# Order of work in an attention loop: the probabilities' transposes a unit later, behind the maxima; the masks' sums behind the normalisation two units back

## The chip, the cores and the metric

The kernel runs on one core of one Trainium2 chip. The metric is the device time of one execution in microseconds (us). A core has four compute engines that work from queues of their own: TensorE (PE in the profile, its weight loads PEld), VectorE (DVE), ScalarE (ACT) and GpSimd (POOL). SyncE (SP) issues all of this kernel's transfers.

## What is computed

Two layers of a gated cross-attention block, on x of shape 8 x 128 x 512 and a context of the same shape. The change lies in the attention of the first layer: 32 heads of width 128, with a position bias per head and a mask per batch.

```
h_q = (rmsnorm(hidden) @ w_q.T).reshape(b, lq, H, DH)      # H = 32, DH = 128
h_k = (context @ w_k.T).reshape(b, lk, H, DH)
h_v = (context @ w_v.T).reshape(b, lk, H, DH)
score = einsum('bqhd,bkhd->bhqk', h_q, h_k) + position_bias[None]
score = where(m, score, -inf)
score = where(m, softmax(score), 0)
attn = einsum('bhqk,bkhd->bqhd', score, h_v).reshape(b, lq, H * DH)
x = x + tanh(g) * (hidden + attn @ w_out.T)
```

After it come a 4-bit quantised dense layer, a second attention of one head and a dense layer with eight low-rank experts.

## The kernel before

The program is unrolled in full. It has three stages. First all keys and queries are projected, pair of heads by pair of heads, and stored in DRAM (to about 350 us). Then comes a loop over 64 units, in which values are projected, attention is done and the output projection is added to x (about 350 to 835 us). Last come the remaining layers, as a pipeline over the eight batches.

A unit is one head and one half of the batch, that is 4 batches: `where(u)` gives head and half. Values (`make_values`, matmuls named c_v at L172 to L174) and output projections (`project_out`, matmuls named pso at the same lines, added into x at L702) are spread over the units as they are needed. For one unit u the attention itself goes like this:

- `fetch(u + 2)` loads the stored queries and keys two units ahead (L552).
- `add_masks(u)`, L615, on GpSimd: the mask (0 or a huge negative number) plus the head's bias into a tile of tag s. There are 3 buffers of s.
- `attend(u - 3)`, L683 on TensorE: probabilities times values for the unit three back; its result is split into two parts on ScalarE (L684) and VectorE (L685).
- `scores(u, s)`: four products of queries and keys (L627, TensorE), their sum with the masks (L628, VectorE), the negated maxima of the rows (L632, VectorE), four exponentials with row sums (L639, ScalarE), the reciprocal and its product with a 0/1 factor, named rs (L644 and L645, VectorE), and the normalisation of the whole tile by rs (L646, GpSimd).
- `move_probs(u)`: the tile goes out to DRAM as through (L657) and comes back in four pieces as moved (L660), with blocks exchanged between partitions. There are 2 buffers of moved.
- `transpose_probs(u - 1)`, L668, on VectorE: each 32 x 32 block of the moved tile is transposed into pT, of which there are 2 buffers. Together with the move this is the transpose of the probabilities.

The engines' queues do not simply follow the program's text. When the program is built, a scheduler with a timeline of its own lays out each engine's queue: among what it holds ready at a moment it takes what stands first in the text. Two tools bend this order. `mark(name, inst)` notes an instruction, and `with behind(name):` makes every instruction in the block queue behind the noted one on the same engine. It adds an order within that queue, no wait for anything else. `in_order` keeps one engine's queue as the text has it; it is used on TensorE around the first and the last stage, not around the units. So the place of `transpose_probs(u - 1)` is: on VectorE, somewhere behind rs of unit u. The mask sums have no such order: a mask sum may be queued as soon as the scheduler sees a buffer of s come free, that is when through of the unit three back has left.

The last attends (units 61 to 63) and the last transpose (unit 63) are in `ending()`, the first of the last stage's steps.

Of the kernel before, what the change touches and what calls it, by code (L numbers as in the profile page):

```python
# [13 lines left out]
ALU = mybir.AluOpType  # L14
AX = mybir.AxisListType

P = 128
# [5 lines left out]
NU = 2 * H  # L23
HALF = NB // 2
BY_PAIR = [b for j in range(HALF) for b in (j, j + HALF)]
NR = 15
Q32 = 32
NQ = P // Q32
# [32 lines left out]
def kernel(  # L61
# [37 lines left out]
    nc = tc.nc  # L99
# [6 lines left out]
    def keep(shape, name, dtype=F32):  # L106
        return sb.tile(shape, dtype, tag=name, name=name)

    def slot(shape, tag, name, dtype=F32):
        return sb.tile(shape, dtype, tag=tag, name=name, bufs=TAGS[tag])  # L110
# [9 lines left out]
    def ptile(shape, tag, name):  # L120
        return psum.tile(shape, F32, tag=tag, name=name, bufs=BANKS[tag])
# [8 lines left out]
    def mark(name, inst):  # L130
        marks[name] = inst.ins

    @contextmanager
    def behind(*names):
        with ExitStack() as stack:
            for name in names:
                stack.enter_context(tc.issue_after(marks[name]))
            yield
# [206 lines left out]
    def load_wo(h):  # L345
        if h < H:
            load(f"wo_{h}", wo[:, h])

    def split_wo(h):
        t = raws.pop(f"wo_{h}")  # L350
        high, low = (wide_row("wo", f"wo_{n}{h}", F32R) for n in "hl")
        split(high, low, t, nc.gpsimd)
        wos[h] = high, low
# [3 lines left out]
    def load_bias(g):  # L357
        if g < NP:
            t = slot([P, 2, P], "bias", f"bias_{g}")
            nc.sync.dma_start(out=t, in_=pbias[:, g * 2 : (g + 1) * 2])  # L360
            biases[g] = t
# [184 lines left out]
    def fetch(u):  # L546
        if u < NU:
            p, r = divmod(u, 4)
            half, i = divmod(r, 2)
            for kind in ("queries", "keys"):  # L550
                t = slot([P, HALF * P], "kq", f"{kind[0]}_{u}")
                nc.sync.dma_start(out=t, in_=stored[kind, p][:, 2 * i + half])  # L552
                fetched[kind, u] = t
# [16 lines left out]
    def by_block(t):  # L570

        return t.rearrange("p b (n k) -> p n b k", k=Q32)
# [3 lines left out]
    mneg = keep([P, 2, NQ, HALF, Q32], "mneg")  # L576
# [27 lines left out]
    def where(u):  # L604

        p, r = divmod(u, 4)
        half, i = divmod(r, 2)
        return 2 * p + i, half

    def add_masks(u):  # L610

        h, half = where(u)
        s = slot([P, NQ, HALF, Q32], "s", f"s_{u}")
        bias = biases[h // 2][:, h % 2, :].rearrange("p (n k) -> p n k", k=Q32)
        nc.gpsimd.tensor_tensor(  # L615
            s, mneg[:, half], bias.unsqueeze(2).to_broadcast([P, NQ, HALF, Q32]), ALU.add
        )
        return s

    def scores(u, s):  # L620
        _, half = where(u)
        q, k = fetched.pop(("queries", u)), fetched.pop(("keys", u))
        bs = slice(half * HALF, (half + 1) * HALF)
        ps = ptile([P, HALF, P], "sc", f"sc_{u}")
        for j in range(HALF):
            cols = bass.ts(j, P)
            nc.tensor.matmul(ps[:, j, :], lhsT=q[:, cols], rhs=k[:, cols], start=True, stop=True)  # L627
        nc.vector.tensor_tensor(s, by_block(ps), s, ALU.add)  # L628
        nm = small.tile([P, HALF], F32, tag="nm", name=f"nm_{u}")
        mark(  # L630
            "max",
            nc.vector.tensor_reduce(  # L632
                nm, s.rearrange("p n b k -> p b n k"), AX.XY, ALU.max, negate=True
            ),
        )
        sm = small.tile([P, HALF], F32, tag="sm", name=f"sm_{u}")
        for j in range(HALF):
            one = s[:, :, j, :]
            e = nc.scalar.activation(  # L639
                one, one, AF.Exp, bias=nm[:, j : j + 1], accum_out=sm[:, j : j + 1]  # L640
            )
        mark("exp", e)
        rs = small.tile([P, HALF], F32, tag="rs", name=f"rs_{u}")
        nc.vector.reciprocal(rs, sm)  # L644
        mark("rs", nc.vector.tensor_tensor(rs, rs, anykey[:, bs], ALU.mult))  # L645
        nc.gpsimd.tensor_tensor(  # L646
            s, s, rs.unsqueeze(1).unsqueeze(3).to_broadcast([P, NQ, HALF, Q32]), ALU.mult
        )
        probs[u] = s

    def move_probs(u):


        s = probs.pop(u)
        moved = slot([P, NQ, HALF, Q32], "moved", f"moved_{u}")
        through = dram.tile([P, NQ, HALF * Q32], F32, tag="through", name=f"through_{u}")
        nc.sync.dma_start(out=through, in_=s.rearrange("p n b k -> p n (b k)"))  # L657
        blocks = through.rearrange("(i q) n f -> n q i f", q=Q32)
        for j in range(NQ):
            nc.sync.dma_start(  # L660
                out=moved[bass.ts(j, Q32)].rearrange("p i b k -> p i (b k)"), in_=blocks[j]
            )
        probs[u] = moved

    def transpose_probs(u):

        t = slot([P, HALF, P], "pT", f"pT_{u}")
        nc.vector.transpose(by_block(t), probs[u])  # L668
        probs[u] = t

    def attend(u):
        h, half = where(u)
        p, i = divmod(h, 2)
        pT = probs.pop(u)
        if i == 0:
            attns[p, half] = page([P, 2, 2, HALF, P], f"a_{p}_{half}")
        a = attns[p, half][:, i]
        ah, al = a[:, 0], a[:, 1]
        cols = bass.ts(i, P)
        av = ptile([P, HALF, P], "av", f"av_{u}")  # L680
        for b in range(HALF):
            v = values_of[p, half, b // 2][:, b % 2, :]
            nc.tensor.matmul(av[:, b, :], lhsT=v[:, cols], rhs=pT[:, b, :], start=True, stop=True)  # L683
        mark("a", nc.scalar.copy(ah, av))  # L684
        nc.vector.tensor_tensor(al, av, wide(ah), ALU.subtract)  # L685
# [19 lines left out]
    def project_out(p, b):  # L705
        half, j = divmod(b, HALF)
        ps = ptile([P, D], "mm", f"pso_{p}_{b}")
        product(
            ps,
            [  # L710
                (tuple(attns[p, half][:, i, part, j, :] for part in range(2)), wos[2 * p + i])
                for i in range(2)
            ],
        )
        add_to_x(b, ps, tgx0, "h1" if p == NP - 1 else None)
# [218 lines left out]
    def make_values(n):  # L934
        nonlocal made
        while made < n:
            next(value_work, None)
            made += 1

    def unit(u):  # L940
        p, r = divmod(u, 4)
        fetch(u + 2)
        if r == 3:
            load_bias(p + 1)
        if r in (0, 1):
            load_wo(2 * p + r)

        n = 2 * (u - OUT_LAG)

        goal = 14 + int(1.74 * (u - 2)) if u > 2 else 0  # L950
        if n >= 0:
            project_out(*divmod(n, NB))
        make_values((made + goal + 1) // 2)
        if n >= 0:
            project_out(*divmod(n + 1, NB))
        make_values(goal)
        s = add_masks(u)
        if u >= LAG:
            attend(u - LAG)
        scores(u, s)  # L960
        move_probs(u)
        if u > 0:
            with behind("rs"):
                transpose_probs(u - 1)
        if r in (2, 3):
            with behind("exp"):
                split_wo(2 * p + r - 2)

    make_values(7)
    unit(0)  # L970
    make_values(11)
    unit(1)
    make_values(14)
    for u in range(2, NU):
        unit(u)
# [299 lines left out]
    def ending():  # L1275

        outs = iter(range(2 * (NU - OUT_LAG), NP * NB))

        def project(n):
            for _ in range(n):  # L1280
                project_out(*divmod(next(outs), NB))

        project(4)
        attend(NU - 3)
        project(1)
        yield
        project(3)
        make_values(14 * (H // 4 + 1) - 3)
        attend(NU - 2)
        yield  # L1290
        make_values(14 * (H // 4 + 1))
        transpose_probs(NU - 1)
        yield
        attend(NU - 1)
        project(4)
        yield

    key, ffn, att, last = ([s(b) for b in range(NB)] for s in (keys, ffn0, xattn1, ffn1))

    starts = [[ending()], ffn[:1], ffn[1:2], ffn[2:3], [ffn[3], key[0]]]  # L1300
    starts += [[ffn[b], key[b - 3]] for b in range(4, NB)]
    starts += [[att[0], key[5]], [att[1], key[6]], [att[2], key[7]]] + [[c] for c in att[3:] + last]
# [76 lines left out]
```

## Time and profile before

| what | value |
|---|---|
| time, median of 3 runs | 973.51 us (970.68 to 974.13) |
| the profiled execution | 976.74 us, of which the span from first to last instruction is 974.9 us |
| matmul clock granted | 0.991 on average |
| DMA, mean over the span | 180 GB/s |
| first and last scores of the loop (L627) | from 350.4 us, unit 63's at 814.2 us |
| transposes (L668) | 64, 0.71 us each, 372.9 to 828.0 us |
| mask sums (L615) | 64, 1.29 us each, 292.5 to 803.6 us |
| normalisations (L646) | 64, 1.04 us each, 360.5 to 820.2 us |
| through<-s, moved<-through | 2.7 and 2.5 us from issue to landing (median) |

The profile is of one execution. A line of it names an engine, a line of the kernel, an operation, and the tiles as out<-in. Behind the bar stand the busy time, the mean length of one instruction in ns, and the idle time of the engine ahead of these instructions with what ended it. In a timeline, the idle time ahead of an instruction and its releaser stand in square brackets.

### The profile page before, as it was taken

What the parts mean: (1) busy time and instruction counts of PE and PEld (TensorE: products, weight loads), DVE (VectorE), ACT (ScalarE), POOL (GpSimd) and SP (SyncE); (2) the same over time, 40 slices, a digit from 0 to 9 for tenths busy, and PEclk for the clock granted to TensorE, in tenths of its full rate; (3) what the DMA queues carried; (4) which work ended last, traced back from release to release, by engine and by line L of the source; (5) the groups of instructions that cost most, each with busy time, mean ns of one, the idle gap of its engine ahead of it and who ended that gap; (6) DMA issues with size and microseconds to landing.
All of it is one profiled execution on the core that took longest, in us unless ns stands there. A gap on an engine that the chain in (4) does not pass through costs nothing. (4 is left out here: it accounts for less than half of the span.)

```text
span 974.9 us, 16587 instructions
## 1 busy us (share of the span) xinstructions
PE 926.1 (95%) x5444; PEld 807.9 (83%) x5444; DVE 651.5 (67%) x1341; ACT 500.0 (51%) x1435; POOL 482.4 (49%) x524
## 2 busy tenths in 40 slices
PE   6989999998999988899999999999999999989998
PEld 4877788887888878799889989898898998878987
DVE  7777766675778944665667576575676577645686
ACT  5565545655564544443434445353552535666761
POOL 4844322112231584763847649376495852553431
PEclk9999999999999999999999999999999999999999
DMA  8544465788886687566665856656575656513001
GB/s 282 176 143 131 141 204 180 229 262 279 275 273 202 200 255 221 156 192 166 178 179 174 222 166 181 195 166 193 160 205 171 174 160 205 216 45 131 1 23 66
DMA packets 125269, 175.00 MB, mean 180 GB/s; under 512 B 17406, under 2 KB 55294, under 8 KB 124030
## 3 DMA queue, kind: packets, MB, share of 16 engines
q1 hardware_dynamic: 125182, 173.94, 58.4%
q8 instruction: 43, 0.70, 0.3%
q14 instruction: 44, 0.36, 0.1%
HBM read 109.85 MB, written 64.03 MB: 178 GB/s over the span
## 5 line engine op out<-in xcount | busy, mean ns | idle before, releaser
L639 ACT ACTIVATE s<-s,nm 128x128 f32<-128x128 f32 x256 | 99.7, 391 | 188.0 <-issue 76.0
L615 POOL TENSOR_TENSOR s<-mneg,bias 128x512 f32<-128x512 f32 x64 | 82.5, 1291 | 87.1 <-DMA through<-s 78.3
L172 PE MATMUL pso<-wo_h,a 128*128 128x512 f32 x256 | 107.2, 419 | 6.1 <-DVE x L702 6.1
L668 DVE STREAM_TRANSPOSE pT<-moved 128x512 f32<-128x512 f32 x64 | 45.4, 710 | 97.7 <-DMA moved<-through 97.4
L174 PE MATMUL pso<-wo_h,a 128*128 128x512 f32 x256 | 101.2, 396 | 1.1 <-DVE a L685 1.1
L173 PE MATMUL pso<-wo_l,a 128*128 128x512 f32 x256 | 101.1, 395 | 0.0
L646 POOL TENSOR_TENSOR s<-s,rs 128x512 f32<-128x512 f32 x64 | 66.6, 1041 | 64.6 <-ACT wo_h L163 18.7
L702 DVE SCALAR_TENSOR_TENSOR x<-pso,tg,x 128x512 f32<-128x512 f32 x128 | 93.4, 738 | 5.7 <-PE pso L174 5.7
L172 PE MATMUL c_v<-wvP,cxT 128*128 128x256 f32 x288 | 82.6, 287 | 0.8 <-ACT v L253 0.7
L173 PE MATMUL c_v<-wvP,cxT 128*128 128x256 f32 x288 | 81.5, 283 | 0.0
L174 PE MATMUL c_v<-wvP,cxT 128*128 128x256 f32 x288 | 81.4, 283 | 0.0
L683 PE MATMUL av<-pT,v 128*128 128x128 f32 x512 | 69.1, 276 | 8.0 <-DVE pT L668 6.0
L683 PEld LDWEIGHTS av<-pT,v 128*128 128x128 f32 x512 | 64.5, 191 | 13.2 <-issue 5.3
L627 PE MATMUL sc<-k,q 128*128 128x128 f32 x512 | 69.9, 279 | 4.2 <-issue 1.6
L627 PEld LDWEIGHTS sc<-k,q 128*128 128x128 f32 x512 | 64.2, 194 | 6.1 <-DVE nm L632 2.9
L172 PE MATMUL c_v<-wvP,cxB 128*128 128x256 f32 x216 | 61.8, 286 | 3.4 <-DVE v L254 2.6
L172 PEld LDWEIGHTS pso<-wo_h,a 128*128 128x128 f32 x256 | 48.5, 189 | 15.2 <-DVE x L702 6.6
L173 PE MATMUL c_v<-wvP,cxB 128*128 128x256 f32 x216 | 61.0, 283 | 0.0
L174 PE MATMUL c_v<-wvP,cxB 128*128 128x256 f32 x216 | 61.0, 282 | 0.0
L164 POOL TENSOR_TENSOR wvP<-raw_wv,wvP 128x512 fp32r<-128x512 f32 x43 | 56.3, 1318 | 7.1 <-ACT wvP L163 7.1
L174 PEld LDWEIGHTS pso<-wo_h,a 128*128 128x128 f32 x256 | 48.0, 188 | 13.0 <-DVE a L685 2.0
L172 PEld LDWEIGHTS c_v<-wvP,cxT 128*128 128x128 f32 x288 | 55.0, 191 | 4.0 <-ACT v L253 1.3
(276 smaller groups left out, 2779.9 us busy)
## 6 DMA issues: line engine op xcount, KB each, us to landing
keys<-keys SPq DMA_DIRECT2D x64, 256.0 KB, 3.4
queries<-queries SPq DMA_DIRECT2D x64, 256.0 KB, 3.9
q<-queries SPq DMA_DIRECT2D x64, 256.0 KB, 4.0
k<-keys SPq DMA_DIRECT2D x64, 256.0 KB, 4.5
through<-s SPq DMA_DIRECT2D x64, 256.0 KB, 2.7
moved<-through SPq DMA_DIRECT2D x256, 64.0 KB, 2.5
raw_wk<-in_wk_dram SPq DMA_DIRECT2D x32, 256.0 KB, 3.9
raw_wq<-in_wq_dram SPq DMA_DIRECT2D x32, 256.0 KB, 4.1
```

The costliest lines, as they stand in the source:

```text
L164: mark("low", (low_engine or nc.vector).tensor_tensor(low, src, wide(high), ALU.subtract))
L172: nc.tensor.matmul(out, lhsT=lh, rhs=rh, start=first, stop=False, **more)
L173: nc.tensor.matmul(out, lhsT=lh, rhs=rl, start=False, stop=False, **more)
L174: nc.tensor.matmul(out, lhsT=ll, rhs=rh, start=False, stop=last, **more)
L615: nc.gpsimd.tensor_tensor(s, mneg[:, half], bias.unsqueeze(2).to_broadcast([P, NQ, HALF, Q32]), ALU.add)
L627: nc.tensor.matmul(ps[:, j, :], lhsT=q[:, cols], rhs=k[:, cols], start=True, stop=True)
L639: e = nc.scalar.activation(one, one, AF.Exp, bias=nm[:, j : j + 1], accum_out=sm[:, j : j + 1])
L646: nc.gpsimd.tensor_tensor(s, s, rs.unsqueeze(1).unsqueeze(3).to_broadcast([P, NQ, HALF, Q32]), ALU.mult)
L668: nc.vector.transpose(by_block(t), probs[u])
L683: nc.tensor.matmul(av[:, b, :], lhsT=v[:, cols], rhs=pT[:, b, :], start=True, stop=True)
L702: "x", nc.vector.scalar_tensor_tensor(xs[b], ps, factor, xs[b], ALU.mult, ALU.add, **out)
```

## The change

The transposes are called a unit later and from inside `scores`: unit u's call follows the maxima of unit u + 2, and has to queue behind them on VectorE. What was called for unit 62 in unit 63 is now called in the ending. The mask sum of unit u has to queue behind the normalisation of unit u - 2 on GpSimd. Nothing is computed otherwise.

```
     def add_masks(u):
...
-        nc.gpsimd.tensor_tensor(
-            s, mneg[:, half], bias.unsqueeze(2).to_broadcast([P, NQ, HALF, Q32]), ALU.add
-        )
+        with behind(*(f"norm{u - 2}",) * (u > 1)):
+            nc.gpsimd.tensor_tensor(
+                s, mneg[:, half], bias.unsqueeze(2).to_broadcast([P, NQ, HALF, Q32]), ALU.add
+            )
         return s
...
     def scores(u, s):
...
         mark("max", nc.vector.tensor_reduce(nm, ..., AX.XY, ALU.max, negate=True))
+        if u > 1:
+            with behind("max"):
+                transpose_probs(u - 2)
         sm = small.tile([P, HALF], F32, tag="sm", name=f"sm_{u}")
...
-        nc.gpsimd.tensor_tensor(
-            s, s, rs.unsqueeze(1).unsqueeze(3).to_broadcast([P, NQ, HALF, Q32]), ALU.mult
-        )
+        factors = rs.unsqueeze(1).unsqueeze(3).to_broadcast([P, NQ, HALF, Q32])
+        mark(f"norm{u}", nc.gpsimd.tensor_tensor(s, s, factors, ALU.mult))
         probs[u] = s
...
         scores(u, s)
         move_probs(u)
-        if u > 0:
-            with behind("rs"):
-                transpose_probs(u - 1)
...
     def ending():
...
         project(3)
+        transpose_probs(NU - 2)
         make_values(14 * (H // 4 + 1) - 3)
         attend(NU - 2)
```

## The prediction

> **What bounds the kernel now.** I read the page's busy table first, then the busy times by stage, then TensorE's waits in the stage that the change touches, and last the timeline of VectorE and GpSimd inside it.
>
> ```profile
> PE 926.1 (95%) x5444; PEld 807.9 (83%) x5444; DVE 651.5 (67%) x1341; ACT 500.0 (51%) x1435; POOL 482.4 (49%) x524
> ...
> L615 POOL TENSOR_TENSOR s<-mneg,bias 128x512 f32<-128x512 f32 x64 | 82.5, 1291 | 87.1 <-DMA through<-s 78.3
> ...
> L668 DVE STREAM_TRANSPOSE pT<-moved 128x512 f32<-128x512 f32 x64 | 45.4, 710 | 97.7 <-DMA moved<-through 97.4
> ```
>
> TensorE is busy nearly all the time and VectorE two thirds of it. The two groups that the change moves are the two that hold their engines longest for a DMA: the mask sums on GpSimd (78.3 us) and the transposes on VectorE (97.4 us). Idle time of an engine that is not the bound is worth nothing by itself; the question is what it does to TensorE. By stage (columns: length, then PE, PEld, DVE, ACT, POOL busy, clock, DMA share, GB/s):
>
> ```profile
> 350.00:400.00 50.00, 41.81 (x306) 38.95 (x304) 23.68 (x48) 25.07 (x88) 30.08 (x26) 0.97 0.78 231
> 400.00:835.00 435.00, 421.54 (x2852) 382.93 (x2853) 287.61 (x516) 197.28 (x655) 269.68 (x235) 1.00 0.62 179
> ```
>
> The units run from about 350 us (scores of unit 0) to 835 us. From 400 to 835 us TensorE is idle 435.00 - 421.54 = 13.5 us. Its waits there add up to exactly that, and all end on VectorE:
>
> ```profile
> PE av L683 <- DVE pT L668: 5.6, 5, 1.3
> PE pso L172 <- DVE x L702: 5.3, 8, 2.7
> PE c_v L172 <- DVE v L254: 2.6, 3, 1.4
> ```
>
> So 13.5 us, 1.4% of the run, is all that a better order of VectorE can win in this stage. One of these waits, read in the timeline of VectorE (columns: start, length, engine, line, operation, count, idle before and who ended it):
>
> ```profile
> 569.37 0.74 DVE L702 SCALAR_TENSOR_TENSOR x<-pso,tg,x 128x512 f32<-128x512 f32 x1
> 572.15 0.71 DVE L668 STREAM_TRANSPOSE pT<-moved 128x512 f32<-128x512 f32 x1 [2.03 <-DMA moved<-through]
> 572.78 0.65 DVE L254 TENSOR_TENSOR v<-c_v,v 128x512 f32<-128x512 f32 x1
> 573.36 0.68 DVE L685 TENSOR_TENSOR a<-av,a 128x512 fp32r<-128x512 f32 x1
> 573.96 0.68 DVE L628 TENSOR_TENSOR s<-sc,s 128x512 f32<-128x512 f32 x1
> ```
>
> and the matmul that paid for it, in TensorE's:
>
> ```profile
> 573.49 0.39 PE L172 MATMUL c_v<-wvP,cxB 128*128 128x256 f32 x1 [1.44 <-DVE v L254]
> ```
>
> The transpose of unit 28 waits 2.03 us for its DMA. The value sum at L254 and unit 30's score sum at L628 stand behind it, although unit 30's scores had been multiplied from 567.5 us on. TensorE waits 1.44 us for the value sum. GpSimd shows the same shape:
>
> ```profile
> 563.75 1.04 POOL L646 TENSOR_TENSOR s<-s,rs 128x512 f32<-128x512 f32 x1 [1.33 <-ACT a L684]
> 566.97 1.27 POOL L615 TENSOR_TENSOR s<-mneg,bias 128x512 f32<-128x512 f32 x1 [2.18 <-DMA through<-s]
> 569.60 1.04 POOL L646 TENSOR_TENSOR s<-s,rs 128x512 f32<-128x512 f32 x1 [1.35 <-ACT v L253]
> ```
>
> The sum at 566.97 is unit 31's mask, three units ahead of the normalisation at 563.75 (unit 28), because the three buffers of tag s make it wait until unit 28's probabilities have left.
>
> **What the Trainium skill says.** "TensorE: Matmul & The Clock Gate", section "Architectural detail: the array is 16× 32×32, not 1× 128×128": VectorE and GpSimd take their instructions strictly in order. The trace agrees: the 2.03 us above. "Perfetto Trace Analysis", section "Identifying the Most-Contended Engine": TensorE's headroom is judged by the weight loads' busy share, not the matmuls'. Here that is 382.93 of 435.00, 88%, so I do not take TensorE's 97% as a wall, only as saying that its queue seldom runs dry. "DMA: Bandwidth & Descriptors", section "Two DMAs through the same engine are not ordered": a DMA that reads what another wrote has to be issued after the first one's semaphore. The trace shows the issuing queue doing so: SyncE's queue waits 84.1 us, 55 times, at L660 for the DMA through<-s between 400 and 835 us. This makes the round trip that a transpose waits for two DMAs long.
>
> **The change, part by part.**
>
> (1) The transposes. The number stays 64, each 0.71 us, all on VectorE. Unit u's moves from behind rs(u+1) to behind the maxima of unit u+2. In the timeline, over units 9 to 61 (the steady ones), the maxima come every 7.4 us. The moved block of unit u has landed on average 11.9 us after the end of u's maxima (0.3 until the exponentials, 1.6 for four of them, 1.0 to rs, 0.7 to the normalisation of 1.04, 0.2 to the issue of through, 3.0 to that of moved, 4.1 to the landing). The old slot, behind rs(u+1), is at 7.4 + 2.9 = 10.3 us, so the transpose is early by 1.6 us on average and VectorE waits. The new slot is at 14.4 us, 2.5 us after the mean landing. Most of the 97 us should go; by the same readings 15 to 30 us stay where landings are late (one in ten lands 15.3 us or more after the maxima).
>
> What that wins on TensorE: the three value waits, 2.6 us, each directly behind a waiting transpose. Of the eight x waits, 5.3 us, one of 2.7 us at 402 us belongs to the start, where DMA landings set the order, and one of 0.6 us at 818 us to the end; 2.0 us are left to win. The five pT waits, 5.6 us, are no matter of slot: the DMA itself was late. Two of them (units 16 and 17, 2.2 us) should shrink as the whole softmax chain moves up when VectorE no longer holds it: I take 1.5. Three (units 34, 42, 50, 3.4 us) follow a pair of scores only 2.3 us apart. There a mask sum (1.3 us each) stands ahead of the late normalisation on GpSimd, as at 604.7 us before the normalisation of unit 34 at 608.7, and the change puts it behind: I take 2.2. Sum won: 2.6 + 2.0 + 1.5 + 2.2 = 8.3 us.
>
> What it costs: the result is needed by attend(u), which TensorE runs just ahead of the scores of unit u+3. Now 2.6 us lie on average between the transpose's end and it; with the new slot less. From the end of the scores of u+2 to attend(u) there are on average 5.8 us. The new path in them is the score sum 0.68, the maxima 0.69 and the transpose 0.71, with 0.1 to 0.15 at each step about 2.4 us, plus whatever else VectorE has in its queue ahead of them. So some 3.4 us of other work fit. I bounded the shortfall from both sides over the 53 units. If the score sum starts within 1.4 us of its matmuls' end (two other operations ahead), 0.2 us of waits in three units. If it starts when it did, less only the idle time of the transpose directly ahead of it, 9.7 us in 11 units (unit 27: transposed by 567.7 us, wanted at 566.6). The second forgets that earlier waits pushed it too: the score sum now comes 4.2 us after the first score matmul, of which 1.1 are the matmuls. I take 3 us, near the lower end, as the waits were what pushed it. Behind the moved transpose stand one x or value sum and rs; rs has 1.6 us of exponentials as cover for its 0.71.
>
> (2) The mask sums. 64 stay, 1.29 us each. Unit u's is put behind the normalisation of u-2, whose unit's maxima come before; the buffer it waits for (unit u-3's) has then been free for some 4 us, so 66 us of GpSimd's waits between 400 and 835 us go. It is wanted by the score sum of u. From the end of normalisation u-2 to that sum there are now 8.6 us on average and 4.1 at the least (unit 34), against 1.3 for the mask: covered, unless splits of weights (1.3 us each) line up three deep. At the start mask 2 moves from 347.8 to behind normalisation 0 (361.5 us) and comes out 0.5 us late for its sum at 362.3; mask 5 likewise 0.8 us. Both sums stand in the stretch up to 400 us whose order the DMAs' landings set, so I take 0, and keep 1.4 as the other end. No queue of SyncE waits for a mask.
>
> (3) The buffers. Block u+2 is moved into the buffer that transpose u frees; its DMA is issued some 7 us after the maxima of u+2, the transpose comes 0.7 us after them: no wait. pT: transpose u needs attend(u-2), a unit earlier. The last two transposes come in the ending; unit 62's now in program order behind three output projections, with its DMA landed at 823.9 us and attend(62) at 832.9: nothing.
>
> Sum: -8.3 + 3 + 0 = -5.3 us. The profiled execution took 976.7 (span 974.9), which would become 971.4; it lay 3.2 above the median of the runs shown, 973.5, for which the same sum gives 968.
>
> **The rivals.** A wash (B): the order edges bind little, or the time won comes back as waits at attend. For it: at units 33, 41, 49 and 57 the transpose already comes after the maxima of u+2 (602 to 611 us: no change there), as in most of the first six units; and the upper bound of the cost, 9.7, against 8.3 won. Against: in the other 49 of 53 units the transpose stands ahead of those maxima. Time 971 to 977, say 974.
>
> Slower (C): TensorE closes a loop. Scores of u+2, their sum, maxima, transpose of u, attend(u), scores of u+3 are one chain now, of 4.3 us without queueing in a period of 7.4. If one VectorE operation more (0.7 us) stands ahead of the sum than in my upper bound, the same reading gives 19.4 us of waits in 17 units, less the 4.6 us of x and value waits won: +15, 988 us; with half of one (0.35 us), 13.8 - 4.6 = +9, 983 us. It decides where the score sum starts on average some 2.2 us or more after its matmuls' end (my upper bound has 1.9; traced are 3.1). For it: VectorE has 3.5 us of other work per unit, and the scheduler that lays out the queues rearranges everything with the edges. Against: this queueing is now made by the very waits that go.
>
> **How the numbers follow.** The forecast (A) 0.60, its own range 963 (10.7 of the 13.5 us won) to 972 (4.6 won, 3 lost). B 0.14. C 0.26, 979 to 990. A measurement tells about 0.5%, 4.9 us, from no change: under 968.6 lie 0.43 of A and 0.01 of B; within 968.6 to 978.4 0.17 of A, 0.11 of B, 0.01 of C; above, 0.25 of C and 0.02 of B. Low end 961, below A's own by what the start might give; high end 985, inside C.
>
> **What would show it.** Right: the wait of the transposes falls from 97 to under 35 us, that of the mask sums to under 15; the score sum starts within 3 us of its first matmul; TensorE's waits for L254 and x after 410 us are gone; waits at attend total 5 us or less. Wrong: attend waits for the transposes in 15 or more units (C), or the transposes keep over 60 us of waits (B). A changed order on TensorE itself, attends behind the next scores, would make the sum above unsafe in both directions.

## The result and the profile after

The changed kernel takes 960.33 us, median of 4 runs (955.06 to 962.43), against 972.18 us (970.68 to 974.13) for the kernel before, measured beside it: 11.9 us less, a ratio of 0.987 with a 95% interval of 0.982 to 0.992. The forecast was 968 from a median of 973.5 then, a gain of 5.3, so the gain has the right sign and is about twice as large as forecast. The profiled execution of the changed kernel took 959.39 us (span 957.6). The pair of profiled executions differs by 17.3 us, 5.5 more than the medians do: the one before lay 4.6 above its median, this one 0.9 below. Differences between the two traces are therefore not a measure of the gain to the microsecond.

The page of the changed kernel, its busy table and the two groups that moved:

```profile
PE 919.2 (96%) x5444; PEld 807.4 (84%) x5444; DVE 650.3 (68%) x1341; ACT 505.9 (53%) x1435; POOL 482.4 (50%) x524
...
L616 POOL TENSOR_TENSOR s<-mneg,bias 128x512 f32<-128x512 f32 x64 | 82.5, 1289 | 26.4 <-DMA through<-s 26.4
...
L671 DVE STREAM_TRANSPOSE pT<-moved 128x512 f32<-128x512 f32 x64 | 45.2, 706 | 46.3 <-DMA moved<-through 46.3
```

Counts and lengths of the instructions are the same as before. The mask sums' wait for a DMA falls from 78.3 to 26.4 us, the transposes' from 97.4 to 46.3. The same stretch of the units as in the prediction, now 13 us shorter (columns as there):

```profile
350.00:400.00 50.00, 43.41 (x304) 41.03 (x303) 29.25 (x55) 25.69 (x89) 27.40 (x24) 0.93 0.74 222
400.00:822.00 422.00, 414.75 (x2848) 381.47 (x2847) 284.13 (x513) 203.33 (x655) 270.20 (x234) 1.00 0.63 188
```

From 400 to 822 us TensorE shows 422.00 - 414.75 = 7.3 us of idle time, where it showed 13.5 before. Again its waits add up to that (columns: engine, line and what it is waiting for; us in total, times, longest):

```profile
PE av L686 <- DVE pT L671: 4.6, 4, 2.1
PE pso L172 <- DVE x L705: 2.0, 1, 2.0
PE c_v L172 <- ACT v L253: 0.7, 1, 0.7
```

The value waits are gone, one x wait near the end of the loop is left, and attends wait 4.6 us instead of 5.6. So the named waits fell by 6.2 us, close to the 5.3 of the forecast, and yet the kernel won about twice that. The timeline of VectorE in the changed kernel, at the place that the prediction showed (L629 is the score sum, L633 the maxima, L671 the transpose):

```profile
573.34 0.69 DVE L688 TENSOR_TENSOR a<-av,a 128x512 fp32r<-128x512 f32 x1 [2.42 <-ACT a L687]
573.95 0.68 DVE L629 TENSOR_TENSOR s<-sc,s 128x512 f32<-128x512 f32 x1
574.80 0.75 DVE L705 SCALAR_TENSOR_TENSOR x<-pso,tg,x 128x512 f32<-128x512 f32 x1 [0.17 <-PE pso L174]
575.47 0.67 DVE L633 TENSOR_REDUCE nm<-s 128x4 f32<-128x512 f32 x1
576.06 0.70 DVE L671 STREAM_TRANSPOSE pT<-moved 128x512 f32<-128x512 f32 x1
```

The transpose of unit 30 follows the maxima of unit 32 without a wait: its block has been there for a while. What VectorE waits for here is an attend's result, which comes when TensorE gets to it and holds nobody up.

GpSimd's timeline in the changed kernel (L651 a normalisation, L616 a mask sum):

```profile
579.70 1.04 POOL L651 TENSOR_TENSOR s<-s,rs 128x512 f32<-128x512 f32 x1 [0.33 <-DVE rs L649]
...
581.95 1.30 POOL L616 TENSOR_TENSOR s<-mneg,bias 128x512 f32<-128x512 f32 x1
...
584.45 1.03 POOL L651 TENSOR_TENSOR s<-s,rs 128x512 f32<-128x512 f32 x1
585.45 1.29 POOL L616 TENSOR_TENSOR s<-mneg,bias 128x512 f32<-128x512 f32 x1
```

Normalisations 32 and 33 are each followed by the mask sum of two units on, 34 and 35, and these find their buffer free.

**Where the rest of the gain was.** The prediction read TensorE's lost time from its idle column. Two matmuls of the kernel before, and the next one, in TensorE's timeline:

```profile
571.42 0.39 PE L173 MATMUL pso<-wo_l,a 128*128 128x512 f32 x1
571.65 0.40 PE L174 MATMUL pso<-wo_h,a 128*128 128x512 f32 x1
573.49 0.39 PE L172 MATMUL c_v<-wvP,cxB 128*128 128x256 f32 x1 [1.44 <-DVE v L254]
```

The first two start 0.23 us apart, although each is shown with 0.39 to 0.40 us: matmuls are pipelined, and 0.23 us is what one of 512 columns costs. The third starts 1.84 us after the second, so 1.61 us are lost, and the idle column says 1.44. Each gap is understated by some 0.17 us (the shown length less the distance), and a gap shorter than that isn't shown at all. I therefore took the usual (median) distance from one start to the next for each kind of matmul (227 ns for 512 columns, 120 for 256, 111 for 128, 122 for 264), which makes about 895 us of issued work in every kernel of this study, and called loss what a stretch of issued work takes beyond that. From 400 to 835 us the kernel before issued 411.1 us of work: its loss is 23.9 us, not 13.5. Of that, 9.6 us lie in 97 gaps of more than 0.05 us that are too short for the idle column. The changed kernel issues the same matmuls with a loss of 12.0. By stretches of issued work, in us (these count work and not time: 400 is reached at 443 us before and 436 after, 750 at 812 and 795):

| stretch of issued work | before | changed |
|---|---|---|
| 0 to 325 (first stage) | 27.6 | 24.6 |
| 325 to 400 (start of the unit loop) | 14.9 | 11.3 |
| 400 to 750 (steady units) | 19.2 | 9.1 |
| 750 to 835 (end of the loop) | 10.2 | 10.0 |
| 835 to the end | 7.5 | 7.2 |

The steady units give 10.1 us and the start of the loop 3.6. The 3.0 us of the first stage aren't the change's: no matmul of it moved, and the other kernels of the study lie between 23.2 and 27.7 there. The granted clock differs there as well, 0.99 before and 1.00 after; at the start of the loop it is 0.98 before and 0.96 after, so it doesn't explain the gain there. In the steady units it is 1.00 in both (columns as above):

```profile
443.00:812.00 369.00, 358.64 (x2443) 326.46 (x2441) 245.09 (x436) 164.61 (x558) 230.52 (x193) 1.00 0.63 180
436.00:795.00 359.00, 354.39 (x2446) 326.66 (x2445) 243.03 (x441) 171.88 (x568) 232.29 (x194) 1.00 0.62 186
```

The first line is before, the second after. Over these same matmuls the idle time falls from 10.4 to 4.6 us, the loss by distances from 19.2 to 9.1.

### The profile page after: what moved, and what is told of

Its sections match the earlier page's. It is cut to its first block, busy times and chain, and to the rows that moved or that the text cites. A ratio compares the mean times of both kernels' runs of the same rounds, so it can differ in the third digit from the quotient of the medians.

```text
span 957.6 us, 16579 instructions
## 1 busy us (share of the span) xinstructions
PE 919.2 (96%) x5444; PEld 807.4 (84%) x5444; DVE 650.3 (68%) x1341; ACT 505.9 (53%) x1435; POOL 482.4 (50%) x524
## 4 chain that ended last, share of the span: by engine, by line
PE 63%; DMA 14%; DVE 11%; issue 4%; POOL 3%; ACT 2%; SPq 2%; DVEq 0%; POOLq 0%; ACTq 0%
PE sc L628 5%; PE pso L174 5%; PE pso L172 5%; PE av L686 5%; PE pso L173 5%; PE c_v L172 4%; PE c_v L173 4%; PE c_v L174 4%; DMA raw_wk<-in_wk_dram 4%; DMA through<-s 4%; PE c_q L172 3%; PE c_q L174 3%; PE c_q L173 3%; DMA moved<-through 2%; PE c_k L172 2%
## 5 line engine op out<-in xcount | busy, mean ns | idle before, releaser
L651 POOL TENSOR_TENSOR s<-s,rs 128x512 f32<-128x512 f32 x64 | 66.7, 1043 | 100.0 <-DVE rs L649 64.5
L616 POOL TENSOR_TENSOR s<-mneg,bias 128x512 f32<-128x512 f32 x64 | 82.5, 1289 | 26.4 <-DMA through<-s 26.4
L628 PE MATMUL sc<-k,q 128*128 128x128 f32 x512 | 73.4, 276 | 6.2 <-DMA k<-keys 6.2
L671 DVE STREAM_TRANSPOSE pT<-moved 128x512 f32<-128x512 f32 x64 | 45.2, 706 | 46.3 <-DMA moved<-through 46.3
L628 PEld LDWEIGHTS sc<-k,q 128*128 128x128 f32 x512 | 66.8, 192 | 8.5 <-issue 3.5
L688 DVE TENSOR_TENSOR a<-av,a 128x512 fp32r<-128x512 f32 x64 | 43.6, 681 | 44.6 <-ACT a L687 44.4
L172 PE MATMUL c_v<-wvP,cxB 128*128 128x256 f32 x216 | 62.6, 290 | 0.0
L687 ACT CAST a<-av 128x512 fp32r<-128x512 f32 x64 | 37.3, 583 | 47.8 <-PE av L686 47.7
L174 PE MATMUL c_v<-wvP,cxB 128*128 128x256 f32 x216 | 61.6, 285 | 0.0
L173 PE MATMUL c_v<-wvP,cxB 128*128 128x256 f32 x216 | 61.6, 285 | 0.0
L629 DVE TENSOR_TENSOR s<-sc,s 128x512 f32<-128x512 f32 x64 | 44.0, 687 | 23.9 <-PE sc L628 12.1
```

Source lines behind the costliest of these rows:

```text
L172: nc.tensor.matmul(out, lhsT=lh, rhs=rh, start=first, stop=False, **more)
L173: nc.tensor.matmul(out, lhsT=lh, rhs=rl, start=False, stop=False, **more)
L174: nc.tensor.matmul(out, lhsT=ll, rhs=rh, start=False, stop=last, **more)
L616: nc.gpsimd.tensor_tensor(s, mneg[:, half], bias.unsqueeze(2).to_broadcast([P, NQ, HALF, Q32]), ALU.add)
L651: mark(f"norm{u}", nc.gpsimd.tensor_tensor(s, s, factors, ALU.mult))
```

## The experiments

All times are medians, and each ratio is to the kernel before timed beside it on the same chip. "Steady loss" is the loss in the stretch from 400 to 750 of issued work, from one profile each. The "slot" is how long after the end of its own unit's maxima a transpose starts, the "landing" how long after them its block has landed, both means over units 12 to 59. The kernel before has slot 12.6 us (with its waits in it), landing 12.1, steady loss 19.2.

**Each part alone, both, and both in the steady units only.** One theory was that the transposes alone bring most of the gain, another that the mask sums do. All four kernels ran on one chip, where the kernel before took 975.58 us.

Transposes alone: the changed kernel, with the mask sums free of any order, as before.

```
-        with behind(*(f"norm{u - 2}",) * (u > 1)):
+        with behind():
             nc.gpsimd.tensor_tensor(
```

> The transposes' move alone, the mask sums free as before. Theory 1 (the gain is that VectorE no longer holds its queue for a DMA, so the transposes carry it): 960 to 965 us, at least three quarters of the gain of the whole change (about 9 of 12 us), transposes' wait on VectorE 40 to 55 us, mask sums' wait on GpSimd still 50 us or more. Rival 2 (GpSimd freed by the masks is what makes the normalisations and so the landings early): 968 us or more. Rival 3 (any new order edge makes the scheduler lay out TensorE's queue anew, and the gain is luck of that layout): anything between 955 and 980, without relation to the waits.

Mask sums alone: the changed kernel with the transposes called as before.

```
-        if u > 1:
-            with behind("max"):
-                transpose_probs(u - 2)
...
+        if u > 0:
+            with behind("rs"):
+                transpose_probs(u - 1)
```

> The mask sums behind the normalisation two units back alone, the transposes behind rs as before. Theory 1: 969 to 973 us, no gain or under 3 us, transposes' wait on VectorE still 80 us or more, mask sums' wait on GpSimd under 35. Rival 2: 960 to 965 us. Rival 3: anything.

Both, which is the changed kernel itself:

> The changed kernel again, beside its parts on the same chip: 958 to 963 us under every theory; it is the scale for the other three.

Both from unit 10's block on (`u > 11` in both places of the change), the start of the loop as before:

> Both parts from the block of unit 10 on; the first ten units transposed behind rs and masked as before. The two traces at hand put some 4 us of the difference between matmul work before about 400 us and the same work after it, in the start of the loop, which was costed at nothing. If that is the change's doing: about 4 us slower than the changed kernel, 963 to 966. If it is the one profiled execution's: within 2 us of the changed kernel, 958 to 962.

| kernel | us | ratio | loss at the start | steady loss | at the loop's end |
|---|---|---|---|---|---|
| before | 975.58 | | 14.9 | 19.2 | 10.2 |
| transposes alone | 972.59 | 0.997 (0.995 to 0.999) | 13.9 | 15.0 | 12.4 |
| mask sums alone | 969.89 | 0.994 (0.993 to 0.996) | 12.0 | 14.7 | 12.0 |
| both | 959.92 | 0.984 (0.981 to 0.987) | 10.9 | 8.4 | 14.8 |
| both, steady units only | 969.93 | 0.994 (0.991 to 0.997) | 14.9 | 7.0 | 12.6 |

(The loss of the kernel before is from its one profile above.) Neither part carries the gain: alone they win 3.0 and 5.7 us, together 15.7, almost twice the sum. And the changed order in the steady units alone does bring the steady loss down, but not the whole time: at 969.93 us it misses both ranges named for it.

The third reading named ahead of these runs, a new layout of TensorE's queue, isn't tested by these four. Over units 12 to 59, the kernel before starts the attend of unit u behind the scores of unit u + 3 in 4 of 48 units, mask sums alone in none, transposes alone in 37, both in 38. So the edge on the transposes changed TensorE's order too, and this order alone isn't enough, as transposes alone has nearly the same count and little of the gain.

Why don't the transposes do it alone? VectorE's and GpSimd's waits in the units say what is late. For transposes alone, whole execution:

```profile
POOL s L616 <- DMA through<-s: 100.7, 36, 5.9
```

```profile
DVE pT L671 <- DMA moved<-through: 65.0, 27, 5.5
```

For mask sums alone, the same:

```profile
DVE pT L668 <- DMA moved<-through: 89.6, 47, 5.0
```

With the mask sums free, they wait more than before (100.7 us), and the moved transposes still wait 65.0 us. The timeline of GpSimd in transposes alone (L616 is a mask sum, L651 a normalisation):

```profile
547.31 1.04 POOL L651 TENSOR_TENSOR s<-s,rs 128x512 f32<-128x512 f32 x1
553.80 1.29 POOL L616 TENSOR_TENSOR s<-mneg,bias 128x512 f32<-128x512 f32 x1 [5.45 <-DMA through<-s]
555.05 1.28 POOL L164 TENSOR_TENSOR wo_l<-raw_wo,wo_h 128x512 fp32r<-128x512 f32 x1
556.28 1.04 POOL L651 TENSOR_TENSOR s<-s,rs 128x512 f32<-128x512 f32 x1
```

and that of VectorE in the same kernel:

```profile
550.97 0.16 DVE L649 TENSOR_TENSOR rs<-rs,anykey 128x4 f32<-128x4 f32 x1
...
557.20 0.71 DVE L671 STREAM_TRANSPOSE pT<-moved 128x512 f32<-128x512 f32 x1 [3.51 <-DMA moved<-through]
...
564.70 0.71 DVE L671 STREAM_TRANSPOSE pT<-moved 128x512 f32<-128x512 f32 x1 [3.44 <-DMA moved<-through]
```

The factors of unit 27 are ready at 551.1. GpSimd stands until 553.8 in the mask sum of unit 29, which wants the buffer of unit 26; the normalisation of 27 starts at 556.28, 5.1 us after its factors. Its block lands accordingly late, and the transpose at 564.70 waits 3.44 us even in its later slot. That mask sum waits for a block's transfer, and delays the next block's: a loop of GpSimd and the DMAs. The time that a mask sum still waited after the next normalisation's factors were ready is 34 us in 20 units here, 10 us in 7 before, and under 2 us, in one unit each, in mask sums alone and in both. The steady loss that transposes alone has over both (15.0 against 8.4) lies where this happens: in the stretch of issued work from 450 to 550 (units 17 to 29) it loses 8.9 us, the kernel before 4.2 and both 1.0. The blocks of these units land 16.2 us after their maxima, in both 12.9. TensorE's only waits in that stretch of transposes alone (490 to 599 us) are for the transposes:

```profile
PE av L686 <- DVE pT L671: 4.9, 6, 2.3
```

The late landings don't fix the size of the loss: in the second profile of steady units only, further below, the blocks of these units land 16.2 us after their maxima as well, and the stretch loses 3.6.

The other way round, mask sums alone keeps the transposes' early slot (11.6 us, landing 11.3), and VectorE waits 89.6 us, nearly as before. So each part alone leaves the transposes waiting, for a different reason.

**A fourth buffer instead of a later mask.** If the loop through the buffers is what matters, one buffer more should do as well. Tag s gets a fourth; to make room, the tags pr and sel shrink from 4 to 1 and 2, and the table `cols` from 60 to 32 columns.

```
-    "page": 14, "v": 15, "wo": 8, "raw": 6, "kq": 6, "s": 3, ...
-    "pr": 4, "sel": 4,
+    "page": 14, "v": 15, "wo": 8, "raw": 6, "kq": 6, "s": 4, ...
+    "pr": 1, "sel": 2,
...
-        with behind(*(f"norm{u - 2}",) * (u > 1)):
+        with behind(*(f"norm{u - 3}",) * (u > 2)):
```

> The transposes moved as in the changed kernel; the mask sum of unit u behind the normalisation of u-3, which is its place in the kernel before, but with a fourth buffer of s, so that it no longer waits for the DMA through of unit u-3 (that of u-4 has left long since). To make room the router's tiles pr and sel have fewer buffers in the last stage. New theory 4 (with three buffers the mask sum waits for the transfer ahead of a normalisation whose factors are ready, and the normalisation starts the next transfer: a loop of GpSimd and DMA that runs at the units' own pace; the second part opens it): 958 to 964 us, mask sums' wait on GpSimd under 25 us, within 3 us of the whole change in the loop. If what matters is the place behind the normalisation itself, or the layout that the scheduler happens to make: 968 us or more, like the transposes alone.

It took 956.89 us where the kernel before took 969.0, ratio 0.988 (0.986 to 0.990), with a steady loss of 4.8. With the mask of u behind the normalisation of u - 3 again, but with a buffer that is mostly free by then, the transposes wait 27 us instead of 36 (units 12 to 59), mask sums 18.1 us instead of 26.4 (whole execution), and the gain is that of the change within the intervals (the change has 0.984 to 0.987 in three comparisons). So it is a matter of the wait, not of the mask's place in the queue.

**A later slot for the transposes.** Unit u's transpose behind rs of unit u + 2, some two microseconds after its maxima, the mask sums as in the change.

```
-        if u > 1:
-            with behind("max"):
-                transpose_probs(u - 2)
...
+        if u > 1:
+            with behind("rs"):
+                transpose_probs(u - 2)
```

> As the changed kernel, but the transposes of unit u-2 stand behind rs of unit u instead of behind its maxima, some 2.7 us later. The prediction's slower rival (the attend of the unit has too little time after its transpose) says TensorE's waits at attend grow from 5 us to 15 us or more, and 968 to 975 us. If the scheduler only puts attends behind more of TensorE's other work: 958 to 964, and VectorE's wait for the moved blocks falls under 30 us.

957.84 us, ratio 0.989 (0.986 to 0.992). The slot is now 16.8 us, the landing 12.4, and VectorE's wait for the blocks 4 us in all. The steady loss falls to 3.2, but the ratio is no better than the change's, so no gain over it is shown. Attends, which must come later, wait little. TensorE's waits for the transposes in this kernel, in the units:

```profile
PE av L683 <- DVE pT L668: 3.0, 3, 1.5
```

The loop that the slower rival feared doesn't close. Attends are issued 20.3 us after their unit's maxima where the change has 18.3 and the kernel before 15.8: the scheduler that lays out TensorE's queue put them behind other work as their transposes came later (behind the scores of u + 3 in all of units 12 to 59, in the change in 38 of 48).

**Attends one unit later.** If attends had been short of time, more distance would win more: `LAG` 4, and in the ending attend 60 between two halves of what was `project(4)`.

```
-LAG = 3
+LAG = 4
...
-        project(4)
+        project(2)
+        attend(NU - 4)
+        project(2)
```

> As the changed kernel, with attend four units back instead of three (LAG 4). It takes away what is left of TensorE's waits for pT, 5 us: 953 to 957 us if these are the rest of the cost; 958 to 964 if their time comes back at other waits (x, the values), or if it is hidden in the order of the queue.

956.77 us, ratio 0.986 (0.984 to 0.989): steady loss 4.9, and 9.0 at the loop's end, where the change loses 10.0 to 14.8 in its three profiles. The time falls in the lower range, but on this chip the kernel before is faster too (969.0), and the ratio shows no gain over the change.

**Mask sums one unit later still.** Behind the normalisation of u - 1 instead of u - 2, to find where the order begins to cost.

```
-        with behind(*(f"norm{u - 2}",) * (u > 1)):
+        with behind(*(f"norm{u - 1}",) * (u > 0)):
```

> As the changed kernel, with the mask sum of unit u behind the normalisation of u-1 instead of u-2, a unit later. It is wanted by the score sum of u about 0.8 us after it can end. Theory 4 says that only a mask sum that waits, or comes late, costs: late here, 965 to 975 us, with waits of the score sum for the mask of 20 us and more. If the masks' place hardly matters: 958 to 964.

1015.64 us, ratio 1.047 (1.045 to 1.050). No mask sum waits any more, and VectorE's score sums wait for the masks:

```profile
DVE s L629 <- POOL s L616: 63.9, 47, 8.6
```

In this kernel normalisation, mask sum, score sum, maxima, exponentials, factors and the next normalisation follow one upon the other, and a unit can't be shorter than that chain: 8.09 us where the change has 7.14 (steady loss 52.1). The slack of the change's mask edge is less than one unit.

**Is the mask hold needed for a loss?** The later slot and the later attends together, the later slot with four buffers, the later slot with mask sums free of order, and, in the changed kernel, the transposes called at their new place but free to be queued anywhere. These ran on one chip (kernel before: 972.98 us).

> The two variants that did best, together: transposes of u-2 behind rs of u, attend four units back, masks behind the normalisation two back. If what each took away is separate: 2 to 4 us under either of them, a ratio to the kernel before of 0.980 to 0.984. If TensorE's loss in the steady part is as good as gone (3 to 5 us in either): the same ratio as theirs, 0.985 to 0.989.

> Transposes of u-2 behind rs of u, with four buffers of s and the mask sums behind the normalisation three back. Same two readings: ratio 0.980 to 0.984 if separate, 0.985 to 0.989 if the steady part has nothing left.

> Transposes of u-2 behind rs of u, mask sums free with three buffers as before. VectorE then hardly waits for a moved block (theory 1 would be content: ratio 0.986 to 0.990, as with the masks' edge). Theory 4: the mask sums still wait for their buffer ahead of ready normalisations on GpSimd, 30 us and more of it, and the ratio stays at 0.993 or above, near the transposes moved alone (0.997).

```
         if u > 1:
-            with behind("max"):
-                transpose_probs(u - 2)
+            transpose_probs(u - 2)
```

> As the changed kernel, with the transposes' call where it is now, behind the maxima in the text, but without the order edge: the scheduler may queue them ahead of the maxima as soon as its own timeline has the block landed. If the edge is what moves them: ratio 0.992 to 0.997, like the masks alone (0.994), and the transposes wait 70 us or more on VectorE. If the call's place in the text is enough: 0.984 to 0.989.

| kernel | us | ratio | slot, landing | VectorE waits for blocks | steady loss |
|---|---|---|---|---|---|
| later slot, `LAG` 4 | 955.15 | 0.980 (0.976 to 0.984) | 17.2, 13.5 | 2 | 3.2 |
| later slot, four buffers | 961.4 | 0.987 (0.983 to 0.991) | 16.9, 13.4 | 5 | 2.8 |
| later slot, masks free | 959.38 | 0.985 (0.981 to 0.989) | 16.9, 13.3 | 4 | 5.2 |
| changed, no edge for transposes | 983.79 | 1.010 (1.006 to 1.015) | 11.9, 11.8 | 95 | 23.2 |

The first lies where separate gains were expected, the second where none was left to win, and the intervals of both reach into the other range. The other two bear on the cause. With the later slot and free masks, where the theory of the loop expected 0.993 or above, the ratio is 0.985, although the mask sums wait as much as in transposes alone:

```profile
POOL s L616 <- DMA through<-s: 101.1, 37, 7.5
```

and mask sums hold up ready normalisations for 50 us in 26 units, yet nothing is lost by it. So the hold isn't harmful in itself, and that theory was too strong: the hold costs only where it pushes a landing past its transpose's slot, and 3.6 us of margin between the two cover it. Without the edge on the maxima the scheduler put the transpose ahead of the maxima of u + 2 in all 48 of units 12 to 59 (before: in 44):

```profile
DVE pT L670 <- DMA moved<-through: 116.8, 54, 5.0
```

The new place in the text alone is worth nothing, and the kernel is 1% slower than before, where 0.992 to 0.997 was expected; what makes it slower than mask sums alone isn't shown. It is the edge that moves the transposes.

Over these kernels and those below, a long wait of VectorE for the blocks (units 12 to 59) mostly goes with a large steady loss: 95 us with 23.2, 77 with 19.2, 73 with 14.7, 72 with 20.4, 36 to 49 with 7.0 to 9.1 (the change and steady units only), 27 with 4.8, 20 with 4.9, 2 to 5 with 2.8 to 5.2. But two break the row: transposes alone, 46 us with 15.0, and the second profile of steady units only, 68 us with 9.3. So the sum of the waits doesn't set the loss. The kernels divide more cleanly by order. Where nearly all transposes stand ahead of the maxima (before, mask sums alone, no edge, blocks 0 to 9 only), the score sum starts 2.8 to 3.1 us after its matmuls' end and 14.7 to 23.2 us are lost; where all stand behind them, 0.3 to 0.5 us and 2.8 to 9.3 are lost, transposes alone excepted (0.75 and 15.0). But TensorE's order divides them in the same way: attends stand behind the scores of u + 3 in at most 4 of 48 units in the first group, in 37 or more in the second. No run moves the attends back and leaves the transposes where they were, so what TensorE's new order does by itself stays open. The kernel with mask sums one unit later has another bound and isn't in this row.

**The start of the loop, and repeats.** The change for blocks 0 to 9 only (`1 < u < 12` for both edges, the old call for `u > 10`), and again steady units only, both, and the later slot with `LAG` 4; one chip, kernel before 971.63 us.

> Both parts of the change for the blocks of units 0 to 9 alone; from unit 10 on transposes behind rs and masks free as before. If the start's own loss is what the change removes there (some 4 us by the profiles): ratio to the kernel before 0.995 to 0.997, TensorE's loss before 400 us of issued work down to about 11 us from 15. If the start decides how the later units run (10 us by the medians): 0.990 or below, or no gain at all since the later units fall back into their waits.

> The kernel of the steady-only run once more, for a second profile: its first was one of its fastest executions (963.6 against a median of 969.9). If the rest, 6 us, is lost in the same start, a slower execution shows a loss of 18 us or more there; if it is lost later or by the first stage, the start stays near 15. Ratio 0.992 to 0.997 either way.

> The changed kernel as the scale for this chip: ratio 0.983 to 0.989.

> The fastest variant so far beside the changed kernel on one chip: 2 to 6 us below it if the steady part's remaining loss (9 against 3 us) is the difference; within 2 us if the first time was the chip's.

| kernel | us | ratio | loss at the start | steady loss | at the loop's end |
|---|---|---|---|---|---|
| blocks 0 to 9 only | 969.22 | 0.998 (0.996 to 1.000) | 8.6 | 20.4 | 9.4 |
| steady units only | 967.31 | 0.996 (0.994 to 0.998) | 17.4 | 9.3 | 14.8 |
| both | 957.66 | 0.986 (0.983 to 0.990) | 10.5 | 7.2 | 12.7 |
| later slot, `LAG` 4 | 954.79 | 0.982 (0.978 to 0.986) | 10.1 | 3.8 | 11.7 |

Each piece does its work where it is: the early part lowers the loss at the start, from 14.9 to 8.6, the steady part the steady loss. But the times don't add: 2.4 and 4.3 us alone, 14.0 together. The profiles show three places where "steady units only" lies behind "both" on this chip: 6.9 us at the start, 2.1 in the steady units, 2.1 at the loop's end. Why the start should lose 14.9 and 17.4 us in the two executions without the early part, and why the loop's end gives back 2 to 5 us in several kernels, these runs don't settle; the kernel before has one profile only, and the granted clock dips in these two stretches in most profiles, while in the steady units it stays at 1.00 in the kernel before and in all three profiles of the changed kernel.

The later slot with `LAG` 4 was the fastest version on both occasions, and beats the kernel before by 1.8 to 2.0%. Against the changed kernel on the same chip it is 2.9 us faster, 0.3%, with overlapping intervals: likely, not shown.

## Why the prediction was right in sign and wrong in size

**The transposes' lateness**, right: the mean landing was late for the old slot. The slot moved to 15.0 us after the maxima (14.4 forecast). But the transposes kept 46.3 us of waits, not under 35, because the landing moved too, from 11.9 to 13.7 us (units 9 to 61), which I had held fixed. The steps of it, in means: through is issued 1.58 us after the normalisation instead of 0.21, and moved 3.79 after through instead of 3.01. SyncE's queue holds them up. Its waits between 400 and 835 us, in the kernel before and in the changed one:

```profile
SPq L660 <- DMA through<-s: 84.1, 55, 4.4
SPq L663 <- DMA through<-s: 148.3, 57, 5.4
```

The queue stands at moved of unit u until through of u has landed, and through of u + 1 stands behind that: of the 27 units (12 to 59) in which through is issued over 0.5 us after the normalisation, in 24 the queue issues a piece of moved in between. I had said that no queue of SyncE waits for a mask; that holds, but the queue's own order is where the price was. The later slot, with its wait of 4 us, shows that more margin takes the rest of the wait away; a gain in time beyond the change's it doesn't show.

**The mask sums' wait**, direction right, 26.4 us instead of under 15: normalisations come unevenly, and a mask sum behind the one of u - 2 still at times finds the buffer of u - 3 in transfer. In the second profile of the changed kernel ("both" in the first group of experiments), normalisations 28 and 29 lie at 551.9 and 555.7, through of 28 is issued only at 553.2, and mask sum 31 waits for it until 558.7.

**The terms of the sum** were near the truth: value waits 2.6 to 0, x waits nearly gone, attend waits 5.6 to 4.6 (the forecast's own terms make 4.9), in all -6.2 against -5.3. The score sum starts 2.29 us after its first matmul instead of 4.27, within the 3 us named. That the totals fit is in part luck. The 3 us of cost stood for VectorE's queue ahead of the score sum, and that queue cost nothing (the score sum starts 0.35 us after its matmuls' end, 3.07 before). Units 16, 17, 34, 42 and 50 no longer wait, but units 35, 43, 44 and 51 do, for transposes that wait 3.9 to 5.1 us for their blocks: late landings, for which the sum had left 1.9 us. The x wait of 2.7 us at 402 us, which the forecast had left standing, is gone as well, against a new one of 2.0 us at 807.

**The step that failed** is the reading of TensorE's idle column as all of its loss: "So 13.5 us, 1.4% of the run, is all that a better order of VectorE can win in this stage." By distance of issue 23.9 us were lost there. The waits named in the sum fell by 6.2 us, as forecast, but over the same matmuls the loss fell from 23.9 to 12.0; in the steady units alone the idle time fell by 5.8 us and the loss by 10.1 (9.1, 8.4 and 7.2 us are left in the three profiles of the changed kernel). So the gains of the sum, taken together, were priced at little more than half of their size. It isn't that the gain passed the cap, 12.0 lies below 13.5: the terms taken out of it were too small.

**A second term was mis-sized**: what the change does at the start of the loop, "so I take 0", left out of the sum but for the range. It measured -3.6 to -4.4 us in three profiles of the changed kernel, and the early part alone brought the start's loss from 14.9 to 8.6. The reason given, a stretch "whose order the DMAs' landings set", doesn't fit the trace before: of 7.9 us of TensorE's waits from 350 to 400 us 0.9 end on a DMA and 5.4 on VectorE. In the changed kernel those on VectorE are nearly gone, and the keys' DMA is what is left (first line before, second after):

```profile
PE sc L627 <- DMA k<-keys: 0.9, 1, 0.9
PE sc L628 <- DMA k<-keys: 6.2, 2, 3.3
```

How the gain of 11.9 us divides between these two terms stays open. By medians the order in the steady units alone won 5.7 and 4.3 us, no more than the forecast, though its profiles show the steady loss down by 10 to 12 us; the rest came only with the start's part.

**The rivals.** A wash is out: 11.9 us are more than the measurement's 4.9. The slower case needed TensorE's queue to stay as it was; the score sum came early, and attends were laid out later as the transposes moved, from 15.8 to 18.3 us after their maxima. The warning that "A changed order on TensorE itself, attends behind the next scores, would make the sum above unsafe" was the right one: that order did change, and with it attends waited no longer for the later transposes (4.6 us in four of them) than before.

**What the two parts do to each other** the prediction touched on only at three units. The runs show it as the centre of the change: a transpose has to have a slot behind its landing, and a mask sum that waits in front of a ready normalisation makes the landing late. Transposes alone hit the second, mask sums alone the first, and a fourth buffer or a later slot makes up for the mask sums' order. How much of this reaches TensorE through VectorE's freed queue, and how much through TensorE's own new order, is argued here and not shown.

## What to carry to other kernels

An instruction that waits for a DMA on an in-order queue should be placed by the measured landing plus a margin for its spread, after asking what the move does to that landing itself; here about 1 us of mean margin still left waits of 36 to 49 us, and about 4 us took nearly all of them away, though no further gain in time was shown for that alone. Where two waits feed one another through buffers, undoing one of them proves little: try each alone, both, and one buffer more. And what a full engine loses is read from the distances between its starts, not from its idle time.

## What the runs showed of the hardware

- Matmuls of 512 columns are issued 227 ns apart and those of 256 columns 120, while their shown lengths are 0.39 and 0.28 us: they overlap, and the idle time between them is short by the difference. The matmuls of 128 columns are issued 111 ns apart, but they aren't of the same kind: scores and attends show two records for each of their products (512 for 256 products), the wider ones one.
- The prediction judged TensorE's headroom by the Trainium skill's "Perfetto Trace Analysis", section "Identifying the Most-Contended Engine", from the weight loads' busy share, which was 88% before and is 381.47 of 422.00, 90%, after. Distances of issue gave a loss of 23.9 us in 435, 5.5%: TensorE was nearer to its limit than the 88% says.
- Issuing takes time in SyncE's queue besides the waits: in the trace of transposes alone the four pieces of one moved transfer hold it for 1.74 us, the one piece of a through for 0.32.
